# A four-layer graph network on one core: the candidate's aggregation side by seven products, and a new plan for the order of all queues

## The chip, the cores and the metric

The kernel runs on 1 core of one Trainium2 chip, in one launch. The metric is device time in microseconds (us), lower is better. Five queues work in it: PE (TensorE, matrix products), DVE (VectorE), ACT (ScalarE), POOL (GpSimd) and SP (SyncE, which issues nearly all transfers). Each executes its own instructions strictly in the order in which the program holds them; between queues only semaphores order the work.

## The reference

128 graphs of 128 nodes with 256 features each, float32, and an integer adjacency matrix per graph. Four layers, each `x = layernorm(x + gnn(x, adj))`:

```python
# layer 0: four edge scores, softmax, weighted sum
alpha = where(adj == k + 1, leaky_relu(einsum('bid,bjd->bij', x * a_k, x)), -9e15)   # k = 0..3
out0 = softmax(alpha) @ x
# layer 1: mean over neighbours
out1 = relu(x @ W_upd + (A^T (x @ W_msg)) / deg + bias)
# layer 2: three steps of a gated unit (GRU), weights w_ih, w_hh of 3 x 256 rows
for i in range(3):
    aggr = A^T (h @ weight[i])
    gi, gh = aggr @ w_ih.T + b_ih, h @ w_hh.T + b_hh
    r, z = sigmoid(i_r + h_r), sigmoid(i_z + h_z)
    n = tanh(i_n + r * h_n)                       # the candidate
    h = (1 - z) * n + z * h
# layer 3: attention with one vector, softmax, elu
out3 = elu(softmax(where(adj > 0, leaky_relu(f_i + f_j), -1e9)) @ (x @ W))
```

## The kernel before

**Work and tiles.** Four graphs make a group of 512 nodes (`G`, `T`), so there are 32 groups. In the three GRU steps the state lies transposed, as two tiles `hT[0]`, `hT[1]` of 128 features x 512 nodes. `weights` sets up: it turns the weights and multiplies `weight[i]` into `w_ih` (`c_gi`), so that aggregation comes first in each step (`aggregate`: 24 small bf16 products of the split state with the 0/1 matrix `a_ne`, copied to `agT` by ScalarE).

**Seven products instead of eight.** A gate (R, Z or the hidden side of the candidate C) is a 256 x 256 matrix times a 256 x 512 state. Read as 2 x 2 blocks, this is eight block products of 256 columns (or four products of 512 columns); `gate` makes it with seven, after Winograd. `sums` makes the four sums of state blocks (`t_h` on GpSimd from the state, `t_m` on VectorE from `agT`), the set-up the sums of weight blocks (`w_sh`, `w_sm`). The seven products accumulate in two PSUM banks: in `shared`, products 1, 6, 7 and 4 are added one after the other into the same columns, and after 1, after 6 and after 7 a `snapshot` copies the columns out before the next product adds to them; `other` holds products 2, 5 and 3. `added` brings snapshot and second bank together. So a gate has turns in which TensorE adds a product, ScalarE copies, and TensorE may go on only after the copy.

**One step** (`step`), in the order of its statements: the hidden side of the candidate `q` (seven products), aggregation, gate R with both sides (14 products, tile `t_r`), the candidate's aggregation side by `direct` (four products of 512 columns into two `ps` banks), `candidate` for the halves 1 and 0, gate Z with both sides (14 products, `t_z`), and `update`, which writes the new state, transposes it through DRAM (`turned`, `back`) and splits it into bf16 parts for the next step. In `candidate`, VectorE multiplies `t_r` by `q` and adds the `ps` bank, ScalarE takes tanh (`t_n`), GpSimd subtracts (`t_d`).

**The order of the queues** is neither the order of the statements nor written out by hand. Every call is recorded as an `Op`, and a planner at the end of the kernel (the loop over `left`, lines 970 to 1007) simulates the five engines with assumed costs and issues one operation after the other: of those that could start, the one with the earliest due time. Costs are the functions `pe_cost` to `pool_cost`, `LANDING` for transfers, and `HOP`, `PE_HOP`, `SLACK` for the way of a result to the next engine. Due times come from `paced`: each stage of group g gets a start and an end in periods (`PERIOD` = 82.744 us). In GRU steps only TensorE's operations spread the due times, and the other engines' are pulled forward by `EAGER`. `holds` models VectorE and GpSimd keeping each other off. The planner also decides when each rotating buffer is taken. All engine instructions are issued at line 232, which is why every row of the profile names L232; one goes by tiles.

**Buffers the change touches.** `h0T` (4 tiles, states from layer 1) and `hT` (6 tiles, states from the steps); `gate` (4 PSUM banks) and `ps` (4 PSUM banks); `w_sm` with sums for two gates.

Of the kernel before, what the change touches and what calls it, by code (L numbers as in the profile page):

```python
# [9 lines left out]
U8 = mybir.dt.uint8  # L10
I32 = mybir.dt.int32
BF16 = mybir.dt.bfloat16
# [6 lines left out]
def kernel(  # L19
# [38 lines left out]
    nc = tc.nc  # L58
# [84 lines left out]
    FAST = ("tensor_scalar", "tensor_scalar_add", "tensor_scalar_mul")  # L143

# [10 lines left out]
    class Op:  # L155
        def __init__(self, engine):
            self.engine, self.calls, self.took, self.landing = engine, [], 0.0, 0.0
            self.after, self.bufs, self.waiting = {}, [], 0
            self.ready, self.nominal, self.urgent = 0.0, 0.0, False
            self.waits = self.holds = False  # L160
            self.rush = 0.0

    class Engine:
# [24 lines left out]
        def __getattr__(self, name):  # L188
            def call(*args, **kw):
                op = self.group or self.record()  # L190
                named = dict(kw)
                out = [named.pop("out")] if "out" in named else [args[0]]
                rest = args if "out" in kw else args[1:]
                if "accum_out" in named:
                    out.append(named.pop("accum_out"))
                out = [v for v in out if isinstance(v, View)]
                ins = [v for v in (*rest, *named.values()) if isinstance(v, View)]
                n = 1
                for v in out + ins:
                    n = max(n, m_of(v))  # L200
                short = self is PE and BF16 in [v.buf.dtype for v in ins]
                op.took += SPLIT if short else self.cost(name, n, "accum_out" in kw)
                op.landing = LANDING if name == "dma_start" else 0.0

                tensors = [v for v in ins if m_of(v) > 4]
                if self is POOL:
                    op.waits, op.holds = True, name == "memset" or len(tensors) > 1
                elif self is DVE and name not in ("transpose", "bn_stats"):
                    op.waits = op.holds = not any(v.buf.pool is psum for v in out + tensors) and (
                        len(tensors) > 1 or (name in FAST and m_of(out[0]) > 4)  # L210
                    )
                for views, writes in ((ins, False), (out, True)):
                    for v in views:
                        whole = v.buf.pool is psum
                        for other, box, wrote in v.buf.accesses:
                            if other is not op and (writes or wrote) and (
                                whole or all(a < d and c < b for (a, b), (c, d) in zip(box, v.box))
                            ):
                                other.after[id(op)] = op
                for views, writes in ((ins, False), (out, True)):  # L220
                    for v in views:
                        v.buf.accesses.append((op, v.box, writes))
                        if v.buf not in op.bufs:
                            op.bufs.append(v.buf)
                            v.buf.left += 1
                op.calls.append((name, args, kw))

            return call
# [10 lines left out]
    LANDING = 4.2  # L239
    HOP = 0.235  # L240
    PE_HOP = 0.55
    SLACK = 0.873

    def pe_cost(op, n, sums):
        return 0.11 if op == "transpose" else 0.222 if n <= P else 0.003 + n / 599.0

    SPLIT = 0.056

    def dve_cost(op, n, sums):
        return 0.14 + n * (0.00056 if op in FAST else 0.00106)  # L250

    def act_cost(op, n, sums):
        return 0.6 if op == "dma_start" else 0.17 + n * 0.001 + (0.2 if sums else 0.0)

    def pool_cost(op, n, sums):
        return 0.2 + n * 0.00266 if op in FAST else 0.55 if op == "memset" else 1.2 if n < 64 else 0.25 + n * 0.0023

# [4 lines left out]
    SP = Engine("SP", nc.sync, lambda op, n, sums: 0.6)  # L262
# [3 lines left out]
    PERIOD = 82.744  # L266
    SPAN = 2.0
    EAGER, RUSH = 5.34, 0.516
    L0_START, L0_END, L1_START, L1_END, L3_START, L3_END = -2.032, -1.293, -0.75, -0.05, 0.173, 0.919
    H_END, M_START, M_END = 0.179, 0.179, 0.503  # L270

    def paced(start, end, pe_only=False):

        took = [op.took if not pe_only or op.engine is PE else 0.0 for op in line]
        total, sofar = sum(took), 0.0
        for op, t in zip(line, took):
            op.nominal = (start + (end - start) * sofar / total) * PERIOD
            op.urgent = pe_only
            sofar += t
        line.clear()  # L280

# [24 lines left out]
    w_sm = tile_of("w_sm", [P, NL, 3, 2, P])  # L306

    def weights():
# [3 lines left out]
        for src, tag, bufs in ((w_ih, "hT", 6), (w_hh, "rest", 4)):  # L312
            for g in range(0, NGC, 2):
                nat = tile_of(tag, [P, 2, D], bufs)
                ACT.dma_start(out=nat, in_=src[g * P : (g + 2) * P].rearrange("(g p) d -> p g d", p=P))
                nats.append(nat)
            if src is w_ih:
                for i in range(NL):
                    w = tile_of("hn", [P, KC, D], 3)
                    ACT.dma_start(out=w, in_=weight[i].rearrange("(c p) e -> p c e", p=P))  # L320
                    wnat.append(w)
        paced(-2.6, -2.5)
        for k, a in enumerate((a0, a1, a2, a3)):
            SP.dma_start(out=acol[:, k, :], in_=a.rearrange("(c p) -> p c", p=P))
        paced(-2.2, -2.1)
# [8 lines left out]
        paced(-2.0, -1.5)  # L334
# [22 lines left out]
        for i in range(NL):  # L357
            wT = tile_of("h0T", [P, KC, D], 4)
# [23 lines left out]
        for n in range(NL + 1):  # L382
            by, gates = POOL if n > 1 else DVE, 3 if n == 0 else 2
            w = [
                (w_hhT[:, k] if n == 0 else c_gi[:, n - 1, k])[:, : 2 * gates * P].rearrange(
                    "p (g e x) -> p g e x", [P, gates, 2, P], g=gates, e=2
                )
                for k in range(KC)
            ]
            w_s = w_sh if n == 0 else w_sm[:, n - 1]  # L390
            a11, a12, a21, a22 = w[0][:, :, 0], w[1][:, :, 0], w[0][:, :, 1], w[1][:, :, 1]
            s2, s3, s4 = [w_s[:, j] for j in range(3)]
            by.tensor_sub(s3, a11, a21)
            by.tensor_add(a21, a21, a22)
            by.tensor_sub(s2, a21, a11)
            by.tensor_sub(s4, a12, s2)
# [22 lines left out]
        paced(-1.9, -0.2)  # L419
# [88 lines left out]
    def loading(g, s):  # L508
# [12 lines left out]
        paced(g - 2.4, g - 2.1)  # L521
        SP.dma_start(out=s.x, in_=x[graphs].rearrange("b n d -> n b d"))
        paced(g - 1.9, g - 1.8)
# [67 lines left out]
    def layer1(g, s):  # L591
# [37 lines left out]
        for c in range(KC):  # L629
            t = tile_of("h0T", [P, T], 4)  # L630
# [12 lines left out]
    def gru(g, s):  # L643
# [5 lines left out]
        def step(i, hT, parts):  # L649
# [16 lines left out]

            def direct(w, v, q, ps=None, of=(0, 1), stop=True):

                start = ps is None
                ps = ps or bank("ps" if q >= C else "gate")  # L670
                with PE:
                    for k in of:
                        PE.matmul(
                            ps, w[:, k, q * P : (q + 1) * P], v[k],
                            start=(start and k == of[0]), stop=(stop and k == of[-1]),
                        )
                return ps
# [25 lines left out]
            def gate(tag, q, sources, copied, added, last=None):  # L703
# [14 lines left out]
                def snapshot(quarter):  # L718
                    copied(t[:, quarter], shared[:, :H], quarter // 2)
                    ops[-1].rush = RUSH  # L720
# [36 lines left out]
            def candidate(c, ps, t, q):  # L757
                DVE.scalar_tensor_tensor(t, t, 1.0, q, op0=OP.add, op1=OP.mult)
                DVE.tensor_add(t, t, ps)
# [6 lines left out]
            def update(c, z, n, d):  # L766

                DVE.scalar_tensor_tensor(d, z, 1.0, d, op0=OP.add, op1=OP.mult)
                new[c] = tile_of("hT", [P, T], 6)
# [12 lines left out]
            at = g + i * SPAN / NL  # L782
# [3 lines left out]
            paced(at, at + H_END, True)  # L786
            aggregate(0)
            aggregate(1)
            paced(at + M_START - 0.03, at + M_START, True)
            of_m = sums(DVE, agT, w_i, w_sm[:, i], agps, "t_m")  # L790
            t0, t1 = gate("t_r", R, (of_h, of_m), copy, DVE.tensor_add, tanh(R))
            n1, d1 = candidate(1, direct(w_i, agT, C + 1), t1, q1)
            n0, d0 = candidate(0, direct(w_i, agT, C), t0, q0)
# [3 lines left out]
            paced(at + M_START, at + M_END, True)  # L797
# [105 lines left out]
    for g in range(NG):  # L903
# [3 lines left out]
        paced(g + L0_START, g + L0_END)  # L907
        layer1(g, s)
        paced(g + L1_START, g + L1_END)
        gru(g, s)  # L910
        if g < NG - 1:
            layer3(g, s, 0, G)
            paced(g + SPAN + L3_START, g + SPAN + L3_END)
        else:

            for b in range(0, G, 2):
                layer3(g, s, b, b + 2)
                paced(g + SPAN + L3_START, g + SPAN + L3_END)
# [29 lines left out]
    def start_of(op):  # L948

        at = op.ready  # L950
        if op.waits:
# [19 lines left out]
    while left:  # L971
        best = None
        for e in engines:
# [5 lines left out]
            if best is None or at < best[0]:  # L979
                op = min(  # L980
                    (op for t, op in starts if t <= at),
                    key=lambda op: op.nominal - (EAGER if op.urgent and e is not PE else 0.0) - op.rush,
# [9 lines left out]
        e.free = at + op.took  # L992
        if op.holds:
            e.held = e.free - 0.14
        end = e.free + op.landing
# [3 lines left out]
        for other in op.after.values():  # L999
            other.waiting -= 1  # L1000
            hop = 0.0 if other.engine is e and not op.landing else SLACK if not other.urgent else HOP
            if hop == HOP and other.engine is PE:
                hop = PE_HOP
            other.ready = max(other.ready, end + hop)
# [31 lines left out]
```

## Time and profile before

| | |
|---|---|
| device time, median of 3 runs | 2764.06 us (2762.44 to 2764.56) |
| span of the profiled execution, first to last instruction | 2761.8 us, 2.3 us below that median |
| mean granted TensorE clock in it | 0.991 |
| busy: PE, DVE, ACT, POOL | 2702.3, 2304.1, 1584.2, 1666.2 us |
| candidate's aggregation side on PE (ps<-agT,c_gi) | 768 instructions of 512 columns |
| candidate's last addition on DVE (t_r<-t_r,ps) | 192 instructions, 131.4 us |

The profile has no device time of its own for the profiled execution; its span is what the rows add up to. A row of a group reads: line, engine, operation, written tile <- read tiles, shape, count, then busy time of all, mean of one in ns, and the idle time of that engine just before them with what ended it. PE is the row of matrix products, PEld that of weight loads; a float32 product counts as two instructions on each. Chain pieces and timeline rows begin with their start and length in us.

### The profile page before, as it was taken

What the parts mean: (1) busy time and instruction counts of PE and PEld (TensorE: products, weight loads), DVE (VectorE), ACT (ScalarE), POOL (GpSimd) and SP (SyncE); (2) the same over time, 40 slices, a digit from 0 to 9 for tenths busy, and PEclk for the clock granted to TensorE, in tenths of its full rate; (3) what the DMA queues carried; (4) which work ended last, traced back from release to release, by engine and by line L of the source; (5) the groups of instructions that cost most, each with busy time, mean ns of one, the idle gap of its engine ahead of it and who ended that gap; (6) DMA issues with size and microseconds to landing.
All of it is one profiled execution on the core that took longest, in us unless ns stands there. A gap on an engine that the chain in (4) does not pass through costs nothing.

```text
span 2761.8 us, 44048 instructions
## 1 busy us (share of the span) xinstructions
PE 2702.3 (98%) x13756; PEld 2138.1 (77%) x13756; DVE 2304.1 (83%) x5108; ACT 1584.2 (57%) x3704; POOL 1666.2 (60%) x1606
## 2 busy tenths in 40 slices
PE   8899999999999999999999999999999999999996
PEld 5677787887887887887887887887887887787774
DVE  5787888888888888888888888888888898888875
ACT  4454665555665655665655665655665655665554
POOL 4544666655666655666655666655676655675542
PEclk9999999999999999999999999999999999999996
DMA  5545555555555556555655556655556555545441
GB/s 121 129 90 99 115 126 129 120 109 124 122 125 131 121 108 129 118 124 133 121 107 127 121 121 134 121 110 123 121 121 134 124 109 120 116 110 118 99 88 43
DMA packets 1397130, 321.88 MB, mean 117 GB/s; under 512 B 1142560, under 2 KB 1388448, under 8 KB 1396896
## 3 DMA queue, kind: packets, MB, share of 16 engines
q1 hardware_dynamic: 1394448, 316.69, 53.7%
q10 hardware_dynamic: 2448, 2.36, 0.3%
q8 instruction: 111, 1.82, 0.3%
q14 instruction: 123, 1.01, 0.1%
HBM read 185.74 MB, written 133.15 MB: 115 GB/s over the span
## 4 chain that ended last, share of the span: by engine, by line
PE 94%; DVE 3%; POOL 1%; ACT 1%; DMA 1%; issue 1%; ACTq 0%; POOLq 0%; DVEq 0%; SPq 0%
PE gate L232 52%; PE ps L232 42%; DVE t_r L232 0%; POOL t_h L232 0%; DVE xb L232 0%; DVE st L232 0%; DMA rest<-in_L_gnn_w_hh_dram 0%; DVE z L232 0%; POOL rstd L232 0%; DMA hn<-in_L_gnn_weight_dram 0%; POOL xa L232 0%; DVE xa L232 0%; DVE t_d L232 0%; POOL t_d L232 0%; DVE hT L232 0%
## 5 line engine op out<-in xcount | busy, mean ns | idle before, releaser
L232 ACT ACTIVATE q<-gate,bhn 128x256 f32<-128x256 f32 x384 | 183.0, 477 | 314.4 <-PE gate L232 313.1
L232 PE MATMUL ps<-agT,c_gi 128*128 128x512 f32 x768 | 356.0, 592 | 0.0
L232 PE MATMUL gate<-t_h,w_hhT 128*128 128x256 f32 x1152 | 345.2, 381 | 5.7 <-ACT t_z L232 4.3
L232 PE MATMUL gate<-t_h,w_sh 128*128 128x256 f32 x1152 | 337.1, 383 | 4.2 <-ACT q L232 1.7
L232 POOL TENSOR_TENSOR rstd<-rstd,neg_half 128x4 f32<-128x4 f32 (+1 forms) x128 | 142.4, 1112 | 218.2 <-DVE rstd L232 215.1
L232 PEld LDWEIGHTS gate<-t_h,w_sh 128*128 128x128 f32 x1152 | 213.7, 191 | 62.8 <-issue 30.4
L232 PEld LDWEIGHTS ps<-xs,xT 128*128 128x128 f32 x2048 | 249.7, 193 | 11.5 <-ACT xs L232 2.6
L232 PEld LDWEIGHTS gate<-t_h,w_hhT 128*128 128x128 f32 x1152 | 211.7, 191 | 56.1 <-issue 16.3
L232 PE MATMUL ps<-xs,xT 128*128 128x128 f32 x2048 | 251.8, 276 | 2.2 <-ACT xs L232 1.3
L232 ACT COPY t_z<-gate 128x256 f32<-128x256 f32 x288 | 107.1, 372 | 244.6 <-PE gate L232 244.0
L232 PE MATMUL ps<-w_um,x1T 128*128 128x512 f32 x512 | 237.1, 595 | 0.2 <-ACT x1T L232 0.2
L232 PEld LDWEIGHTS ps<-agT,c_gi 128*128 128x128 f32 x768 | 145.8, 190 | 114.5 <-issue 106.0
L232 PE MATMUL gate<-agT,c_gi 128*128 128x256 f32 x768 | 229.2, 380 | 2.6 <-ACT agT L232 2.6
L232 PE MATMUL gate<-t_m,c_gi 128*128 128x256 f32 x768 | 228.5, 379 | 0.0
L232 PE MATMUL gate<-t_m,w_sm 128*128 128x256 f32 x768 | 228.4, 379 | 0.0
L232 PE MATMUL gate<-hT,w_hhT 128*128 128x256 f32 x768 | 222.8, 385 | 5.6 <-DVE hT L232 5.6
L232 POOL TENSOR_SCALAR mk<-a_f 128x512 uint8<-128x512 f32 x128 | 201.3, 1579 | 12.2 <-DVE alpha L232 6.6
L232 ACT ACTIVATE xs<-xT,acol 128x512 f32<-128x512 f32 x256 | 182.1, 717 | 40.9 <-PE ps L232 31.5
L232 POOL MEMSET hu<- 128x1 f32 x128 | 10.3, 96 | 303.8 <-DVE fac L232 224.5
L232 DVE TENSOR_TENSOR t_z<-gate,t_z 128x256 f32<-128x256 f32 x192 | 104.2, 543 | 101.4 <-ACT t_z L232 53.7
L232 POOL TENSOR_TENSOR t_d<-h0T,t_n 128x512 f32<-128x512 f32 x64 | 82.9, 1295 | 174.0 <-ACT t_n L232 171.1
L232 PEld LDWEIGHTS gate<-hT,w_hhT 128*128 128x128 f32 x768 | 141.8, 191 | 48.1 <-issue 23.6
(197 smaller groups left out, 7280.1 us busy)
## 6 DMA issues: line engine op xcount, KB each, us to landing
way_h<-z SPq DMA_DIRECT2D x190, 256.0 KB, 2.4
hn<-way_h SPq DMA_DIRECT2D x760, 64.0 KB, 2.4
way<-z SPq DMA_DIRECT2D x126, 256.0 KB, 3.2
x_blocks<-in_x_dram SPq DMA_DIRECT2D x256, 64.0 KB, 2.3
x_in<-in_x_dram SPq DMA_DIRECT2D x32, 512.0 KB, 3.8
way_x<-xb SPq DMA_DIRECT2D x32, 512.0 KB, 2.9
way_p<-z SPq DMA_DIRECT2D x62, 256.0 KB, 2.6
probT<-way_p SPq DMA_DIRECT2D x248, 64.0 KB, 2.3
```

The lines of the kernel that those rows point to most:

```text
L232: getattr(self.engine, name)(*[a.real() if isinstance(a, View) else a for a in args], **{k: a.real() if isinstance(a, View) else a for k, ...
```

## The change

- The candidate's aggregation side is made by `gate` with the seven products, from the sums `t_m` that gates R and Z use. It gets a tile `t_i` (four quarters of 256 columns) and two banks of `gate`, in place of `direct` and its two banks of `ps`. `w_sm` gets sums for the third gate.
- Its snapshots are ScalarE copies; its two inner additions are on VectorE.
- The candidate's last addition, `t_r` + `t_i`, moves from VectorE to GpSimd, except in the last group.
- States of layer 1 and of the steps share one pool of 9 tiles (`hT`) in place of 4 and 6.
- The planner gets other costs for every operation, other hops and margins, other due times for each stage, and a table of shifts for the first and the last six groups. It now tells when an engine is free (`took`) from when a result is there (`lasts`), and any operation that is not a holder no longer waits for the other engine's hold.

```diff
-    LANDING = 4.2
-    HOP = 0.235
-    PE_HOP = 0.55
-    SLACK = 0.873
-    def pe_cost(op, n, sums):
-        return 0.11 if op == "transpose" else 0.222 if n <= P else 0.003 + n / 599.0
-    SPLIT = 0.056
-    def act_cost(op, n, sums):
-        return 0.6 if op == "dma_start" else 0.17 + n * 0.001 + (0.2 if sums else 0.0)
...
+    LANDING = {"e": 5.66, "adj_in": 4.0, "x_in": 3.85, "x1T": 3.53, "way_1": 3.2, "way_2": 3.0, "xc": 3.6, "way_f": 2.0}
+    def pe_cost(op, n, out, ins, pointers, sums):
+        split = any(v.buf.dtype == BF16 or v.steps[-2:-1] == (("bitcast", (BF16,), {}),) for v in ins)
+        took = 0.11 if op == "transpose" else 0.056 if split else 0.005 + m_of(out[0]) / 600.0
+        return took, took + 0.165
...
+    def act_cost(op, n, out, ins, pointers, sums):
+        if op == "dma_start":
+            return 0.6, 5.0
+        lasts = 0.162 + n * 0.00083 + 0.1 * pointers
+        return lasts - 0.104 + (0.12 if sums else 0.0), lasts + (0.11 if sums else 0.0)
...
-    PERIOD = 82.744
-    SPAN = 2.0
-    EAGER, RUSH = 5.34, 0.516
-    L0_START, L0_END, L1_START, L1_END, L3_START, L3_END = -2.032, -1.293, -0.75, -0.05, 0.173, 0.919
-    H_END, M_START, M_END = 0.179, 0.179, 0.503
+    PERIOD = 81.79179
+    EAGER, RUSH = 5.2738, 1.1029
+    HOP, PE_HOP, SLACK, DMA_SLACK = 0.0939, 0.1018, 0.3009, 1.3133
+    TIMES = {
+        "loading": ((-269.2967, -216.6761), (-147.1123, -150.2193),),
+        "layer0": ((-168.1668, -107.0143),),
+        "layer1": ((-61.9931, -4.1582),),
+        "step0": ((2.1812, 23.4244), (7.0732, 27.4940), (15.2942, 41.6915),),
+        "step1": ((54.2807, 63.4509), (58.3678, 71.2000), (69.7980, 95.8240),),
+        "step2": ((108.6644, 125.1873), (123.1454, 127.3808), (118.2039, 151.9648),),
+        "layer3": ((179.8737, 241.5870),),
+    }
+    HEAD = (
+        (-59.717, -8.177, -28.638, -27.470, -4.121, 7.325, -10.397),
...
+    TAIL = (
+        (15.020, 3.976, 3.394, 9.445, 1.940, 13.363, 1.456),
...
-    w_sm = tile_of("w_sm", [P, NL, 3, 2, P])
+    w_sm = tile_of("w_sm", [P, NL, 3, 3, P])
...
-            t = tile_of("h0T", [P, T], 4)
+            t = tile_of("hT", [P, T], 9)
...
-            def direct(w, v, q, ps=None, of=(0, 1), stop=True):
...
-            def candidate(c, ps, t, q):
+            def candidate(c, aggregated, t, q):
                 DVE.scalar_tensor_tensor(t, t, 1.0, q, op0=OP.add, op1=OP.mult)
-                DVE.tensor_add(t, t, ps)
+                (DVE if g == NG - 1 else POOL).tensor_add(t, t, aggregated)
...
-                new[c] = tile_of("hT", [P, T], 6)
+                new[c] = tile_of("hT", [P, T], 9)
...
             t0, t1 = gate("t_r", R, (of_h, of_m), copy, DVE.tensor_add, tanh(R))
-            n1, d1 = candidate(1, direct(w_i, agT, C + 1), t1, q1)
-            n0, d0 = candidate(0, direct(w_i, agT, C), t0, q0)
+            i0, i1 = gate("t_i", C, (of_m,), copy, DVE.tensor_add)
+            n1, d1 = candidate(1, i1, t1, q1)
+            n0, d0 = candidate(0, i0, t0, q0)
...
-        if op.waits:
+        if op.holds:
             at = max(at, (POOL if op.engine is DVE else DVE).held)
...
+        end = at + op.lasts + (DMA_SLACK if op.dma else 0.0)
         if op.holds:
-            e.held = e.free - 0.14
-        end = e.free + op.landing
+            e.held = at + op.lasts - 0.12
...
-            hop = 0.0 if other.engine is e and not op.landing else SLACK if not other.urgent else HOP
-            if hop == HOP and other.engine is PE:
-                hop = PE_HOP
-            other.ready = max(other.ready, end + hop)
+            to_pe = other.engine is PE
+            if e is PE and to_pe:
+                ready = e.free
+            elif e is other.engine and not op.dma:
+                ready = end
+            else:
+                ready = end + (SLACK if not other.urgent else PE_HOP if to_pe else HOP)
+            other.ready = max(other.ready, ready)
```

## The prediction

> **What bounds the kernel now.** I read the page first (busy time, slices, chain), then the busy time stretch by stretch, then the chain in order of time, then the timeline of TensorE, then the groups by shape, then the waits.
>
> ```profile
> span 2761.8 us, 44048 instructions
> PE 2702.3 (98%) x13756; PEld 2138.1 (77%) x13756; DVE 2304.1 (83%) x5108; ACT 1584.2 (57%) x3704; POOL 1666.2 (60%) x1606
> ...
> PE 94%; DVE 3%; POOL 1%; ACT 1%; DMA 1%; issue 1%; ACTq 0%; POOLq 0%; DVEq 0%; SPq 0%
> ```
>
> 98% busy alone could hide waits, and 83% on VectorE is not far off. The busy time by stretches (columns: PE, PEld, DVE, ACT, POOL, clock, DMA share, GB/s) settles it:
>
> ```profile
> 0.00:85.00 85.00, 69.44 (x368) 51.03 (x369) 52.48 (x132) 36.28 (x78) 45.42 (x56) 0.98 0.59 132
> ...
> 1020.00:1360.00 340.00, 340.00 (x1774) 272.37 (x1773) 294.12 (x652) 202.59 (x473) 218.14 (x209) 1.00 0.57 121
> ...
> 2700.00:2762.00 62.00, 36.12 (x135) 25.18 (x135) 33.43 (x87) 29.15 (x76) 11.71 (x12) 0.72 0.13 35
> ```
>
> All six stretches from 340 to 2380 us read 340.00 of 340.00 on PE, at a granted clock of 1.00: 2040 us without an empty moment. What PE lacks lies at the ends: 22.5 us before 340 (340 - 317.5) and 37.2 us after 2380 (382 - 344.8). The chain in order of time gives the period of one group, by the same run of 28 product instructions in neighbouring groups:
>
> ```profile
> 1016.82 6.04 PE gate L232 x28
> ...
> 1099.49 6.04 PE gate L232 x28
> ```
>
> The period is 82.67 us and one 256-column product instruction takes 6.04 / 28 = 0.2157 us. The timeline gives the 512-column one, start to start:
>
> ```profile
> 1411.76 1.88 PE L232 MATMUL ps<-w_um,x1T 128*128 128x512 f32 x4
> 1413.48 0.59 PE L232 MATMUL gate<-t_h,w_hhT 128*128 128x256 f32 x2
> 1413.91 1.88 PE L232 MATMUL ps<-w_um,x1T 128*128 128x512 f32 x4
> 1415.62 0.59 PE L232 MATMUL gate<-t_h,w_sh 128*128 128x256 f32 x2
> ```
>
> 1.72 and 1.71 us for four, so 0.429 us each (the 0.59 us behind a pair of 256 contains the drain, which the next product covers). So in the middle the time is the number of product instructions times these pitches, and nothing else.
>
> **The products.** Each float32 product is two instructions. The candidate's aggregation side was 4 products of 512 columns per step: 8 x 0.429 = 3.43 us. It becomes 7 of 256: 14 x 0.2157 = 3.02 us. That is 0.41 us less per step, 1.24 us per group (period 82.67 to 81.43) and, over 96 steps, 768 x 0.429 - 1344 x 0.2157 = 329.5 - 289.9 = 39.6 us. 2040 / 82.67 = 24.7 of the 32 groups lie where PE is full (30.5 us certain); the other 9 us count where PE is busy, 92% of both ends (662 of 722 us). I take **-39 us**, bounds -30.5 and -39.6. That smaller products might be held up by their weight loads is excluded by the groups: the loads take 0.19 us each and the 28 in a row above still ran at 0.2157.
>
> **The other engines.** The rows by shape:
>
> ```profile
> L232 ACT COPY t_r<-gate 128x256 f32<-128x256 f32 x288 | 107.6, 374 | 91.5 <-PE gate L232 86.0
> L232 DVE TENSOR_TENSOR t_r<-t_r,ps 128x512 f32<-128x512 f32 x192 | 131.4, 684 | 8.3 <-PE ps L232 0.6 <-PE gate L232 0.5
> L232 DVE TENSOR_TENSOR t_r<-gate,t_r 128x256 f32<-128x256 f32 x96 | 39.3, 409 | 25.8 <-ACT t_r L232 24.4 <-PE gate L232 1.2
> L232 POOL TENSOR_TENSOR t_d<-hT,t_n 128x512 f32<-128x512 f32 x128 | 163.3, 1295 | 21.0 <-ACT t_n L232 21.0
> L232 DVE SCALAR_TENSOR_TENSOR t_r<-t_r,q 128x512 f32<-128x512 f32 x192 | 133.0, 693 | 13.3 <-ACT t_r L232 13.3
> L232 DVE SCALAR_TENSOR_TENSOR t_d<-t_z,t_d 128x512 f32<-128x512 f32 x192 | 174.4, 920 | 3.0 <-ACT t_z L232 3.0
> ```
>
> ScalarE gains 4 snapshots a step: 384 x 0.374 = 144 us, per period 49.2 + 12 x 0.374 = 53.7 of 81.4 us. VectorE loses 192 additions of 0.684 (131 us) and gains 96 of 0.409, 96 of about 0.69 and the last group's 6: 109.6 us; per period 71.5 to 70.8. GpSimd gains 186 additions at the 1.295 us of its nearest row: 241 us, 53.0 to 60.8 per period. None reaches 81.4, so all this hides under PE.
>
> GpSimd's additions touch VectorE all the same. The two last rows are the same operation on the same size in SBUF, 693 and 920 ns, and GpSimd works beside both: VectorE is held up at places by 0.2 us. If the 114 us by which the affected rows (t_d, the new hT, the second split) stand above 0.69 us grow with GpSimd's time (241 / 1666), that is 16 us, 0.5 per period. The Trainium skill ("SBUF — State Buffer", section "Who interferes with whom") speaks against the move: a GpSimd operation that reads SBUF and a VectorE one with two SBUF inputs lock each other out for a whole instruction. By that rule up to 7.8 us per period would be added to VectorE. With or without it, the worst case by rows, every one of 6 x 1.295 us standing still on VectorE, is 78.6 of 81.4: still not the bound, so 0 in the sum, but near enough to be a rival below.
>
> **The longer chain.** Candidate: VectorE multiply, GpSimd addition (+0.61 us against VectorE), ScalarE tanh, GpSimd subtraction; two halves, so GpSimd is taken 4 x 1.295 = 5.2 us. The z gate, 14 products of both sides, that is 28 instructions and 6.04 us on PE, stands beside it, and the update needs z anyway. Cost 0 in the middle; at the ends, where PE does wait, at most 0.61 x 2 halves x 3 steps = 3.7 us. Behind a GpSimd addition that waits for VectorE stand the next sums t_h and the powers of the normalisations; GpSimd now waits 218 us in front of those powers, so it has the room. The third gate's table in the set-up makes 12 operations half longer again (8 on GpSimd, 0.72 us before), under 4 us; 9 state buffers instead of 4 + 6 can hold VectorE's state write, where the row of hT shows 2.3 us idle in all: 0 taken, to 5. SP's transfers are the same in number and size.
>
> **The order.** The planner's costs and due times change all queues, and this decides the rest. In the listing of both programs' order with their waits, I took each product that waits for a ScalarE snapshot of the bank it adds to, and summed the TensorE work between the product snapshotted and the waiting one. Before, 49 such turns have 0.87 us or less: one in each middle period, 0.87 each, and the rest at the ends. After, there are 280: t_i 75, t_r 77, t_z 59, q 69. Six of these, with 0.43 or 0, lie in the middle. What a turn needs, the timeline shows near the end, where PE waits:
>
> ```profile
> 2694.37 0.63 PE L232 MATMUL gate<-t_h,w_sh 128*128 128x256 f32 x1
> 2695.04 0.47 ACT L232 ACTIVATE q<-gate,bhn 128x256 f32<-128x256 f32 x1 [2.28 <-PE gate L232]
> 2695.57 1.22 PE L232 MATMUL gate<-t_h,w_sh 128*128 128x256 f32 x2 [0.56 <-ACT q L232]
> ```
>
> The product ends at 2695.00 and the next starts at 2695.57. With the drain (0.59 - 0.43 = 0.16) a turn needs 0.72 us for q, and 0.62 for a 0.374 us copy. 0.86 is enough by 0.14 to 0.24 us if ScalarE is free at that moment. The six without cover cost 2 us (two at 0.62 and 0.72, four at 0.2 to 0.3). For the 226 more turns at 0.86: nothing each, if they go like the 25 before, which cost no slice of the middle anything; or, if ScalarE (66% taken, a mean instruction of 0.43 us) is met at random, 0.66 x 0.25² / (2 x 0.43) = 0.048 us, 11 us; or 0.66 x (0.72 - 0.24) each, 72 us, if a 0.72 us tanh always stands ahead. I take 5, nearer to the row of before, and with the six **+7 us**. At the ends, 14 turns have no cover after and 15 before: I take 0, bounds -25 and +15.
>
> **Sum.** 2761.8 - 39 + 7 = 2729.8 us of span. The median of the runs is 2764.06, 2.3 above the profiled span; with it, **2732 us**.
>
> **Rivals.** (A, 0.62) PE stays full, as summed: 2732, between 2715 and 2750. (B, 0.15, slower) ScalarE's queue becomes the clock: a snapshot stands behind a tanh that waits for VectorE. Rows for it: ScalarE idles 71.0 us before 96 such tanh of t_r, 0.74 each. If a third of the 226 turns lose that, it is 75 x 0.74 = 55 us: 2764 - 39 + 2 + 55 = 2782. It decides from 0.16 us per turn (37 / 226). Against it: the 25 tight turns of before. (C, 0.14) The new order also fills the ends; if it takes 25 of the 59.7 us that PE is empty there, 2707. Against it: as many uncovered turns there. (D, 0.09) GpSimd's additions make VectorE late: at 78.6 of 81.4 us each late result costs PE 0.7 us per period, 2755. That the products are not fewer is excluded by the listing (1344 instructions for 768).
>
> **How the numbers follow.** This kernel's measurement tells 0.2%, 5.5 us. Faster: A, C and half of D, 0.81. Same: some of D and of B's lower end, 0.06. Slower: 0.13. The range 2700 to 2768 takes in A, most of C, all of D and leaves out most of B.
>
> **What would show it.** Right: stretches in the middle again full on PE, equal runs 81.4 us apart, no group ps<-agT,c_gi, GpSimd t_r<-t_r,t_i x186 near 1.3 us, waits of PE gate for t_i, t_r, t_z and q below 20 us together. Wrong: middle stretches short of full, with PE waiting for ScalarE (B) or VectorE (D); or ends that differ by over 15 us (C).

## The result and the profile after

The changed kernel takes 2773.7 us (median of 6 runs, 2769.1 to 2774.8) against 2764.3 for the kernel before, measured beside it (6 runs, 2762.4 to 2765.4): a ratio of 1.003, interval 1.0019 to 1.0042. It is slower by 0.3%, where 2732 was forecast, with a range of 2700 to 2768. All issuing is at line 228 now, so the rows name L228.

The page of the kernel after (span, busy time, chain):

```profile
span 2771.3 us, 45549 instructions
PE 2689.0 (97%) x14332; PEld 2235.5 (81%) x14332; DVE 2211.5 (80%) x5114; ACT 1698.1 (61%) x4088; POOL 1929.6 (70%) x1792
...
PE 67%; DVE 15%; POOL 6%; ACT 4%; DMA 3%; issue 3%; SPq 2%; DVEq 0%; POOLq 0%; ACTq 0%
```

PE is busy for less time and the span is longer. The chain left PE: 94% of it was PE's before, 67% now, with 15% on VectorE. The same three stretches (PE, PEld, DVE, ACT, POOL, clock, DMA share, GB/s):

```profile
0.00:85.00 85.00, 69.12 (x357) 51.42 (x358) 49.60 (x129) 34.87 (x75) 45.71 (x55) 0.98 0.57 128
...
1020.00:1360.00 340.00, 334.28 (x1808) 281.40 (x1807) 275.62 (x642) 211.77 (x513) 246.01 (x229) 0.99 0.57 121
...
2700.00:2772.00 72.00, 41.28 (x154) 28.99 (x154) 36.14 (x97) 33.98 (x88) 18.12 (x19) 0.71 0.20 47
```

The middle is no longer full: over its six stretches PE is busy 2015.2 of 2040 us, where it was 2040.0.

**A better measure than busy time.** A product's record goes on for its drain, 0.16 us past the start of the next product, so a gap shorter than that does not show as idle. I went over the trace from start to start: each product's start, less the start of the product before it, less that one's pitch (0.216, 0.429, 0.056 us for a bf16 one); what is over is a late start. Between 340 and 2380 us these sum to 8.4 us before (150 steps from a bf16 to a float32 product at 0.056 each, no wait) and 58.5 us after: 99 products that wait for another engine, 38.2 us; in 101 cases the second instruction of a late product, 0.104 us in most, 10.7 us in all; and 9.6 us of type steps and small change, about 1 us of it products at half the granted clock (below).

This closes the account. All products at their pitches are 2679.3 us before and 2639.5 after (-39.8). What the spans hold beyond is 82.5 and 131.8 us (+49.3), of which the middle is 8.4 and 58.5 (+50.1) and the two ends together 74.1 and 73.3 (-0.8). So the products bring what was forecast, the ends change nothing in sum, and the middle gives back 50 us.

By the engine whose result let the late product go, the waits in the middle are: VectorE 20 us, ScalarE 11, GpSimd 7. The answer for the waits of PE on the gates (us, times, longest) shows the part of it that is visible as idle:

```profile
PE gate L228 <- DVE t_r L228: 6.3, 6, 2.6
PE gate L228 <- POOL t_h L228: 5.7, 10, 0.8
PE gate L228 <- ACT q L228: 4.6, 7, 1.2
PE gate L228 <- ACT t_z L228: 4.2, 9, 0.8
PE gate L228 <- DVE q L228: 4.0, 8, 0.9
```

No single engine is behind it. Behind one of the longest stands a chain, in the timeline of the kernel after, around 1180 us:

```profile
1180.46 0.69 DVE L228 TENSOR_TENSOR rest<-hn 128x512 f32<-128x512 f32 x1 [2.82 <-DMA hn<-way_h]
...
1183.03 0.42 DVE L228 TENSOR_TENSOR hu<-ps,bias_row 128x256 f32<-128x256 f32 x1
1183.36 0.68 DVE L228 TENSOR_REDUCE nmax<-alpha 128x4 f32<-128x512 f32 x1
1183.95 0.42 DVE L228 TENSOR_TENSOR t_r<-gate,t_r 128x256 f32<-128x256 f32 x1
...
1184.43 0.79 PE L228 MATMUL gate<-hT,w_sh 128*128 128x256 f32 x1 [2.64 <-DVE t_r L228]
```

Read it from below. Product 3 of gate R, which goes into the same columns of `other` as products 2 and 5, waits 2.64 us until VectorE has added snapshot and bank together (`added`; t_r<-gate,t_r). That addition had its inputs by 1180.47, when ScalarE's snapshot was done, 3.5 us before it began. But VectorE executes in order, and it had stood still for 2.82 us (from 1177.64) at the split of a state that was not yet back from DRAM; all that the plan had put between split and addition came late by that. The wait costs more than itself: from 1183.88 us the granted clock is 0.5 for 3.4 us, and the next products start 0.427 us apart where 0.216 is usual, some 1.4 us more. A stretch (its clock is the third number from the end) and two rows of the timeline show it:

```profile
1183.00:1187.00 4.00, 2.57 (x6) 2.13 (x7) 3.35 (x15) 2.90 (x11) 4.00 (x4) 0.61 0.22 35
...
1185.44 1.06 PE L228 MATMUL gate<-agT,w_sm 128*128 128x256 f32 x2
...
1187.65 0.59 PE L228 MATMUL gate<-t_m,c_gi 128*128 128x256 f32 x2
```

The SP queue shows why the split was late:

```profile
1170.58 3.14 SPq L228 DMA_DIRECT2D rT<-way  x2
1173.83 0.50 SPq L228 DMA_DIRECT2D x_in<-in_x_dram  x1
1174.43 2.87 SPq L228 DMA_DIRECT2D hn<-way_h  x4
1177.40 1.12 SPq L228 DMA_DIRECT2D way_h<-z  x1
```

The four issues of `hn` alone take 2.87 us, behind others in the same queue, and VectorE is at the split before the last has landed. By its numbers the new plan allows a part of `hn` 3.7 us from its planned issue (2.4 for the landing and 1.31 of `DMA_SLACK`), and 96 of the 760 took longer in the trace; the plan of before allowed 4.8 (0.6 and 4.2), and 7 took longer. Over the whole kernel the split shows what was new in the row that had no idle time before (busy, mean ns, idle time before it); with it the other rows that the prediction had costed:

```profile
L228 DVE TENSOR_TENSOR rest<-hn 128x512 f32<-128x512 f32 x128 | 101.6, 795 | 13.6 <-DMA hn<-way_h 13.3
L228 POOL TENSOR_TENSOR t_r<-t_r,t_i 128x512 f32<-128x512 f32 x186 | 245.4, 1332 | 106.0 <-ACT t_i L228 73.0
L228 ACT COPY t_i<-gate 128x256 f32<-128x256 f32 x384 | 142.5, 371 | 92.0 <-PE gate L228 87.1
L228 DVE SCALAR_TENSOR_TENSOR t_d<-t_z,t_d 128x512 f32<-128x512 f32 x192 | 166.5, 875 | 45.9 <-ACT t_z L228 33.9 <-POOL t_d L228 8.0 <-POOL t_h L228 3.9
```

Following each of the 99 waits back through what its releaser had waited for, 16.9 of the 38.2 us end at a late `hn`, 17.6 at TensorE itself (turns that the order made too tight) and 3.7 stayed unresolved. This is argued from the trace; e6 below tests the part of `hn`, and nothing tests the other two apart.

### The profile page after: what moved, and what is told of

It reads as the page before. It is cut to its first block, busy times and chain, and to the rows that moved or that the text cites. A ratio compares the mean times of both kernels' runs of the same rounds, so it can differ in the third digit from the quotient of the medians.

```text
span 2771.3 us, 45549 instructions
## 1 busy us (share of the span) xinstructions
PE 2689.0 (97%) x14332; PEld 2235.5 (81%) x14332; DVE 2211.5 (80%) x5114; ACT 1698.1 (61%) x4088; POOL 1929.6 (70%) x1792
## 4 chain that ended last, share of the span: by engine, by line
PE 67%; DVE 15%; POOL 6%; ACT 4%; DMA 3%; issue 3%; SPq 2%; DVEq 0%; POOLq 0%; ACTq 0%
PE gate L228 45%; PE ps L228 22%; SPq L228 2%; DMA hn<-way_h 2%; DVE z L228 2%; DVE rest L228 2%; DVE st L228 1%; POOL t_r L228 1%; DVE t_d L228 1%; DVE t_r L228 1%; DVE hT L228 1%; DVE xb L228 1%; POOL t_h L228 1%; POOL t_d L228 1%; DVE t_m L228 1%
## 5 line engine op out<-in xcount | busy, mean ns | idle before, releaser
L228 PE MATMUL gate<-t_h,w_hhT 128*128 128x256 f32 x1152 | 347.4, 385 | 11.3 <-ACT t_z L228 3.5
L228 PE MATMUL gate<-t_h,w_sh 128*128 128x256 f32 x1152 | 344.7, 384 | 5.5 <-ACT q L228 2.5
L228 PE MATMUL gate<-t_m,w_sm 128*128 128x256 f32 x1152 | 340.2, 380 | 3.1 <-DVE t_m L228 1.6
L228 PE MATMUL gate<-t_m,c_gi 128*128 128x256 f32 x1152 | 341.8, 379 | 0.2 <-ACT t_i L228 0.2
L228 PE MATMUL gate<-agT,c_gi 128*128 128x256 f32 x1152 | 337.3, 381 | 1.3 <-DVE q L228 0.7
L228 PE MATMUL gate<-hT,w_hhT 128*128 128x256 f32 x1152 | 331.3, 382 | 3.2 <-DVE hT L228 1.6
L228 POOL TENSOR_TENSOR t_r<-t_r,t_i 128x512 f32<-128x512 f32 x186 | 245.4, 1332 | 106.0 <-ACT t_i L228 73.0
L228 POOL TENSOR_TENSOR rstd<-rstd,neg_half 128x4 f32<-128x4 f32 (+1 forms) x128 | 150.3, 1175 | 240.5 <-DVE rstd L228 221.6
L228 POOL TENSOR_TENSOR t_d<-hT,t_n 128x512 f32<-128x512 f32 x192 | 254.3, 1337 | 26.8 <-ACT t_n L228 24.5
L228 PEld LDWEIGHTS gate<-t_h,w_hhT 128*128 128x128 f32 x1152 | 206.2, 190 | 72.4 <-issue 26.3
L228 PEld LDWEIGHTS ps<-xs,xT 128*128 128x128 f32 x2048 | 250.0, 194 | 12.0 <-ACT xs L228 2.3
L228 PE MATMUL ps<-xs,xT 128*128 128x128 f32 x2048 | 254.5, 278 | 3.1 <-DVE xa L228 1.1
L228 PEld LDWEIGHTS gate<-t_h,w_sh 128*128 128x128 f32 x1152 | 210.9, 190 | 56.3 <-issue 14.6
L228 PEld LDWEIGHTS gate<-t_m,w_sm 128*128 128x128 f32 x1152 | 218.0, 190 | 39.1 <-ACT t_i L228 4.4
L228 PEld LDWEIGHTS gate<-hT,w_hhT 128*128 128x128 f32 x1152 | 215.4, 191 | 37.8 <-issue 4.2
L228 PEld LDWEIGHTS gate<-t_m,c_gi 128*128 128x128 f32 x1152 | 218.3, 190 | 34.1 <-issue 2.6
L228 PEld LDWEIGHTS gate<-agT,c_gi 128*128 128x128 f32 x1152 | 217.1, 190 | 35.4 <-DVE q L228 2.8
L228 ACT ACTIVATE q<-gate,bhn 128x256 f32<-128x256 f32 x384 | 182.0, 474 | 95.7 <-PE gate L228 91.4
L228 PE MATMUL ps<-w_um,x1T 128*128 128x512 f32 x512 | 239.3, 593 | 0.6 <-DVE xb L228 0.6
L228 POOL TENSOR_SCALAR mk<-a_f 128x512 uint8<-128x512 f32 x128 | 209.5, 1643 | 22.6 <-DVE alpha L228 14.7
L228 ACT ACTIVATE xs<-xT,acol 128x512 f32<-128x512 f32 x256 | 178.2, 719 | 67.7 <-PE ps L228 49.8
L228 DVE SCALAR_TENSOR_TENSOR t_d<-t_z,t_d 128x512 f32<-128x512 f32 x192 | 166.5, 875 | 45.9 <-ACT t_z L228 33.9
```

The source lines that it names most:

```text
L228: getattr(self.engine, name)(*[a.real() if isinstance(a, View) else a for a in args], **{k: a.real() if isinstance(a, View) else a for k, ...
```

## The experiments

My theory after the result: the products are cheaper as computed, and the order of the queues loses the 50 us, by results that reach TensorE a little late. Rivals put the loss on one thing: on the addition on GpSimd, on transfers that the planner thinks too fast, on the hops and margins (0.09 to 0.30 us, where 0.24 to 0.87 stood), or on the seven products themselves, under any order. Ratios below are against the kernel before, run beside each.

**The new work under the old plan.** Kernel before, with the third gate by seven products and one pool of 9 states; last addition on VectorE (e1), and on GpSimd (e2):

```diff
+            i0, i1 = gate("t_i", C, (of_m,), copy, DVE.tensor_add)
-            n1, d1 = candidate(1, direct(w_i, agT, C + 1), t1, q1)
+            n1, d1 = candidate(1, i1, t1, q1)
...
-                DVE.tensor_add(t, t, aggregated)
+                (DVE if g == NG - 1 else POOL).tensor_add(t, t, aggregated)   # e2 only
...
```

> The kernel before with its own plan, and the candidate by seven products (i gate, snapshots on ScalarE), last addition on VectorE, one pool of 9 states (two pools do not fit beside the new tile). Theory M (the new plan leaves too little margin: the 50 us by which products start late in the middle of the changed kernel come from its order): the middle stretches are full again, 2764 - 39 = about 2726 us. Theory P (the products themselves: three more turns per step through four banks and ScalarE stall TensorE under any order): about 2770. Theory G (the addition on GpSimd makes GpSimd and then VectorE late): it is absent here, 2726.

> As e1, with the last addition on GpSimd as in the changed kernel, still with the plan of before. Theory M: like e1, about 2727 us. Theory P: about 2770. Theory G: e1 plus the 40 to 50 us, about 2770, with TensorE waiting for t_h of GpSimd and for VectorE.

Measured: e1 2815.3 (1.0189, 1.0172 to 1.0206), e2 2863.0 (1.0359, 1.0344 to 1.0374). The seven products, planned with the old costs, lose 51 us, and 99 with the addition on GpSimd. No theory had e1 above 2770. Late starts in the middle are 77.8 and 117.7 us, and the ends grow by some 20 and 29 us. The 48 us from e1 to e2 are what the theory of the addition on GpSimd (G) had named, but the order was made anew between them too, so they don't tell the addition from the order. The old plan could not carry the seven products, and the new plan is worth 89 us to the work of the changed kernel (2863.0 to 2773.7).

**The old work under the new plan** (e3): the changed kernel with `direct` and the last addition on VectorE, as before. The weight block of the third gate holds a sum for the seven products, so the candidate's numbers are others; amount and kind of work are those of the kernel before, but for the third gate's sums in the set-up and the one pool of 9 states.

```diff
-            i0, i1 = gate("t_i", C, (of_m,), copy, DVE.tensor_add)
-            n1, d1 = candidate(1, i1, t1, q1)
+            n1, d1 = candidate(1, direct(w_i, agT, C + 1), t1, q1)
...
```

> The changed kernel with its new plan and pool, but the candidate's aggregation side by four products of 512 columns and the last addition on VectorE, as before. Theory M: the late starts stay, 2764 + 40 = about 2805 us, PE short of full in the middle. Theory P and theory G: they go, about 2764 us, PE full.

Measured: 2786.6 (1.0081, 1.0066 to 1.0096). The work of the kernel before, in an order made with the new plan's numbers, takes 22 us more than in its own: 41.8 us of late starts in the middle for 8.4, less 11 us at the ends. The rival that the products alone are at fault falls: the new plan makes late starts with the old work too. They are other ones, though. Some 15 us of the waits are for ScalarE's t_z, which lets go 2.3 us of them in the changed kernel.

**The margins** (e4), and **the margin of transfers alone** (e8):

```diff
-    HOP, PE_HOP, SLACK, DMA_SLACK = 0.0939, 0.1018, 0.3009, 1.3133
+    HOP, PE_HOP, SLACK, DMA_SLACK = 0.235, 0.55, 0.873, 1.3133   # e4
+    HOP, PE_HOP, SLACK, DMA_SLACK = 0.0939, 0.1018, 0.3009, 2.7   # e8
```

> The changed kernel with one line altered: the planner's HOP, PE_HOP and SLACK back to 0.235, 0.55 and 0.873 us (new costs and due times kept). Theory M: the turns get cover, most of the 50 us in the middle go, 2725 to 2735 us. Theory P and theory G: 2770 or more, TensorE late as before.

> The changed kernel with one number of the planner altered: the allowance on top of a transfer's landing (DMA_SLACK) 2.7 instead of 1.3133 us, which is about what the plan of before allowed; a new order follows. Theory T: the late starts go, 2740 or less. Theory G: no difference, 2773. Theory Q: the order is another one with its own uncovered turns, anywhere from 2755 to 2800, with the late starts on other lines.

Measured: e4 2794.7 (1.011, 1.0095 to 1.0125), e8 2795.1 (1.0112, 1.0097 to 1.0127), both 21 us slower than the changed kernel, about half of it in the middle and half at the ends. The theories of margins (M, for e4) and of transfers (T, for e8) had 2740 or less. The waits of VectorE for `hn` in e8:

```profile
DVE rest L228 <- DMA hn<-way_h: 0.3, 1, 0.3
```

13.3 us of such waits are down to 0.3, exactly as meant, yet the late starts in the middle rise from 58.5 to 68.4: the order that comes out has other tight turns (ScalarE's t_z 11 us, GpSimd's t_h 10). A number changed in the planner changes the place of everything; it doesn't take away one wait. So neither run tells what a margin is worth, and the next three keep the order of the changed kernel fixed and change only what runs in it.

**The order kept, the addition back on VectorE** (e5). It is planned for GpSimd and issued on VectorE:

```diff
-                getattr(self.engine, name)(
+                getattr(getattr(op, "on", self).engine, name)(
...
                 (DVE if g == NG - 1 else POOL).tensor_add(t, t, aggregated)
+                ops[-1].on = DVE
```

> The changed kernel with every queue's order kept as it is (the planner still counts the addition as GpSimd's), but the candidate's last addition issued on VectorE at the same place. Theory G (the addition on GpSimd makes t_h and with it TensorE late, and holds VectorE up): the middle loses 20 us or more of its 50, 2750 or less. Theory T (transfers: the turned state lands late, and VectorE's split at the head of its queue keeps the gates' inner additions back): no gain, 2770 to 2780. Theory Q (queues: many small latenesses of all helpers, each met by an order without cover): a few us either way, 2765 to 2780.

Measured: 2774.8 (1.004, 1.0025 to 1.0055): the same as the changed kernel, with the late starts (56.5 us) too. The engine of the addition does not decide the time, in this order. VectorE's own operations do feel it: t_d, 875 ns in the changed kernel, has here

```profile
L228 DVE SCALAR_TENSOR_TENSOR t_d<-t_z,t_d 128x512 f32<-128x512 f32 x192 | 161.1, 846 | 45.1 <-ACT t_z L228 34.7 <-POOL t_d L228 5.1 <-POOL t_h L228 4.0
```

**The order kept, no split of a step's state behind a transfer** (e6): the splits for steps 2 and 3 read the state as VectorE wrote it, in place of its turned copy, so the numbers are others. All transfers are still made; the first step still has its state through DRAM. **Both** (e7).

```diff
-                ap = getattr(ap, name)(*a, **k)
+                ap = a[0].memory().rearrange("p (b n) -> p b n", b=G) if name == "other" else getattr(ap, name)(*a, **k)
...
-                    split_up[c] = split(turning[c], DVE)
+                    h = turning[c]
+                    split_up[c] = split(View(h.buf, h.shape, h.box, (("other", (new[c].buf,), {}),)), DVE)
```

> The changed kernel with every queue's order kept, but the splits of steps 1 and 2, and the aggregation behind them, read the state where VectorE wrote it and not the turned one that comes back through DRAM; the transfers still take place, and nothing but layer 3 waits for them. The aggregation of steps 2 and 3 is then made on the state not turned. Theory T: most of the 50 us go, 2735 or less. Theory Q: what the trace traces back to late transfers goes, 17 of 38 us of waits and their follow-ons, about 2750. Theory G: under 10 us, 2765 or more.

> e5 and e6 together, order kept, with e6's change of the aggregation's input. Theory T: as e6. Theory G: as e5 or below. Theory Q: the sum of both differences, about 2750, and still 20 us of late starts in the middle that neither transfer nor GpSimd's addition explains.

Measured: e6 2755.5 (0.9971, 0.9959 to 0.9983), e7 2764.8 (1.0001, 0.9992 to 1.0011). The stretch of e6 that read 334.28 on PE in the changed kernel:

```profile
1020.00:1360.00 340.00, 337.67 (x1842) 283.60 (x1841) 276.92 (x641) 217.04 (x526) 251.87 (x234) 1.00 0.58 122
```

Late transfers cost the changed kernel 18 us by the medians and 14 between the two profiled runs (2771.3 and 2757.4), where the tracing back gave 16.9. The waits let go by VectorE's t_r and q (with the short operation fac behind them) fall from 16.7 to 7.4 us, though VectorE's own work is the same: that part was the transfers' doing. Some 44 us of late starts stay. In e7 the addition on VectorE costs 9 us that it did not cost in e5, so the two effects do not add up; which result then comes late I have not traced.

**Other orders of the same work.** If the order is the cause, other numbers in the planner must move the time with the work unchanged. e9 is the changed kernel with the addition on VectorE, planned anew; e10 and e11 are e9 with other numbers; e12 is the work of the changed kernel to the instruction (addition on GpSimd) with other numbers:

```diff
-    PERIOD = 81.79179
-    EAGER, RUSH = 5.2738, 1.1029
-    HOP, PE_HOP, SLACK, DMA_SLACK = 0.0939, 0.1018, 0.3009, 1.3133
+    PERIOD = 81.8532   # e10; e11 82.9083; e12 83.0
+    EAGER, RUSH = 7.3065, 1.0538   # e11 7.7613, 1.2976; e12 7.4261, 1.4511
+    HOP, PE_HOP, SLACK, DMA_SLACK = 0.1521, 0.0977, 0.2421, 1.8593   # e11 0.0777, 0.1915, 0.1, 1.6359; e12 0.0722, 0.2481, 0.2312, 1.6359
...
-                (DVE if g == NG - 1 else POOL).tensor_add(t, t, aggregated)   # not e12
+                DVE.tensor_add(t, t, aggregated)
```

> The changed kernel with the last addition on VectorE, and the planner knowing it, so that a new order follows from the same numbers. Theory G (GpSimd's addition is the cost): 2750 or less. Theory Q (an order without cover, whatever the engines): 2755 to 2790.

> The same work as e9 (seven products, last addition on VectorE) in another order: the planner's numbers are EAGER 7.3065, RUSH 1.0538, PERIOD 81.8532 and HOP, PE_HOP, SLACK, DMA_SLACK 0.1521, 0.0977, 0.2421, 1.8593; costs and due times as in the changed kernel. Theory Q: the products' 39 us are there to be had once the helpers' gate work is pulled forward and transfers get more allowance; 2725 to 2750, with under 30 us of late starts in the middle. Theory P2 (three more turns per step lose what seven products gain, in any order): 2760 or more, the late starts on other lines.

> As e10 with a second set of numbers: EAGER 7.7613, RUSH 1.2976, PERIOD 82.9082, margins 0.0777, 0.1915, 0.1000, 1.6359. Theory Q: 2725 to 2755. Theory P2: 2760 or more.

> As e10 with the last addition on GpSimd, as in the changed kernel, and numbers that suit it: EAGER 7.4261, RUSH 1.4511, PERIOD 83.0, margins 0.0722, 0.2481, 0.2312, 1.6359. Theory Q: 2735 to 2765, between e10 and the changed kernel. Theory P2: 2765 or more. Theory G: 2770 or more.

| | median us | ratio, interval | late starts 340 to 2380 us | of it waits |
|---|---|---|---|---|
| before | 2764.4 | 1 | 8.4 | 0 |
| after | 2773.7 | 1.003 (1.0019 to 1.0042) | 58.5 | 38.2 (99) |
| e9 | 2778.2 | 1.005 (1.0035 to 1.0065) | 59.6 | 40.3 (93) |
| e10 | 2744.2 | 0.9927 (0.9912 to 0.9942) | 32.9 | 20.8 (64) |
| e11 | 2756.0 | 0.9969 (0.9957 to 0.9981) | 44.0 | 25.8 (83) |
| e12 | 2753.7 | 0.9961 (0.9947 to 0.9975) | 48.8 | 30.3 (107) |

e12 against the changed kernel is the plain test: the same instructions in another order, 20 us less. e9 against e10 is the other: 34 us less. Not all of it lies in the middle: between the profiled runs it is 16 us for e12, 10 in the middle and 6 or 7 at the ends, and 32 for e10, 27 and 5. And no order of the seven products that ran has less than 32.9 us of late starts, 24.5 more than before. So the order is shown to move 20 to 34 us; that the rest of the 50 can be had by an order too is not shown. e10 beats both kernels, by 20 us (0.7%) and by 29 us. Its page:

```profile
span 2742.8 us, 45630 instructions
PE 2676.5 (98%) x14332; PEld 2239.9 (82%) x14332; DVE 2318.8 (85%) x5300; ACT 1712.5 (62%) x4088; POOL 1711.9 (62%) x1606
...
PE 78%; DVE 12%; POOL 3%; DMA 3%; ACT 2%; issue 2%; SPq 1%; DVEq 0%; POOLq 0%; ACTq 0%
```

The split of the turned state in e10:

```profile
L228 DVE TENSOR_TENSOR rest<-hn 128x512 f32<-128x512 f32 x128 | 93.1, 728 | 0.0
```

And its chain of waits, the same run of 46 product instructions in neighbouring groups:

```profile
1006.61 9.93 PE gate L228 x46
...
1088.63 9.93 PE gate L228 x46
...
1170.63 9.93 PE gate L228 x46
```

VectorE never waits for `hn` there, and the order repeats from group to group, 82.0 us apart. In the chain of the changed kernel over the same 250 us no run of this length comes back. e10 keeps 19 of the 39.8 us by its span (2761.8 to 2742.8): 24.5 us are still lost in the middle, and the ends are 4 us shorter than before. VectorE, at 85%, is busier in e10 than in the changed kernel and still holds TensorE up less.

## Why the prediction was wrong

- **What bounds the kernel before**: right. There is not one wait in 2040 us, by starts too.
- **The products, -39**: right; -39.8 by pitches in the trace. That no product would be held up by a weight load held only where products follow each other without a wait (last section).
- **The other engines, 0**: the busy times came near the sums, but "so all this hides under PE" did not follow from them (the order, below). GpSimd's additions took the 1.3 us assumed (1332 ns). ScalarE and VectorE stayed below PE. One pool of 9 states did not hold VectorE's state write up: 1.0 us of idle time stands before the row of hT, 2.3 before. The 16 us by which GpSimd's additions were to lengthen VectorE's rows are there, when the order is kept: from the changed kernel to e5, all VectorE operations on 128x512 with two inputs in SBUF (the moved addition apart) take 23 us less, and the mean of t_d goes from 875 to 846 ns. That t_d had 920 ns before, with less work on GpSimd, shows that the order moves these rows as well. The rule of the Trainium skill ("SBUF — State Buffer", section "Who interferes with whom"), by which a GpSimd operation that reads SBUF and a VectorE one with two inputs in SBUF lock each other out, agrees with the changed kernel's trace: t_d, the new hT and t_r<-t_r,q took 0.64 to 0.71 us in the 155 cases with no GpSimd operation beside them, and 0.84 in the mean, up to 1.80, in the other 421. In time, the move is worth nothing in this order (e5), and in e7 the addition on VectorE costs 9 us.
- **The ends, 0**: right, -0.8, for this order; in other orders they moved by -11 (e3) to +29 us (e2).
- **The order, +7**: this is the step that failed. It measured +50. I had counted one kind of turn, product to ScalarE snapshot to next product. Those cost 10 to 11 us in all. That this is my bound by random meeting is luck: it was some 33 waits of 0.3 us, where the formula has a short delay at over a third of 226 turns. The test named for them held: PE's waits for ScalarE's t_i, t_r, t_z and q are 11.6 us, below 20. What was missing: turns over two engines, where product 3 waits for VectorE's inner addition and VectorE stands behind something else (20 us); GpSimd's sums t_h, first in the next step (7 us); the second halves of late products (11 us); and transfers. I had put SP's transfers at nothing since their number was the same, while the plan shortened the margin for their landing. e6 prices that at 14 to 18 us, most of it within VectorE's 20.
- **A, full in the middle**: fell. **B** said slower at 2782 by a queue that is late, and the sign and size came near by luck: the queue was VectorE's with transfers at its head, not ScalarE's behind a tanh. **C**: the ends did not fill. **D**: that VectorE is late was right, but not by GpSimd's additions (e5).
- **The error in method**: "PE was full before, so 25 tight turns cost nothing, so 226 will cost little" took a property of the old order for one of the turns. In the old order every result was in time. e3 shows that the same work loses 22 us in an order by the new plan. The listing of waits had shown that everything moved; of the many kinds of turn in it I counted the one that the change names.

What stays open: which order would have no late start with the seven products, if there is one (by the account it would take about 2725 us, 2764 less 39.8); which of the planner's many new numbers (costs, holds, due times, margins) made the turns tight, as each run that changed one made a whole new order; and why e6 and e5 together (e7) are worse than e6.

## What to carry to other kernels

When a change comes with a new order of in-order queues, cost the order first: list every kind of wait that ends at the bounding engine, over one and over two engines and over transfers, and look for how early each result is, not only for whether the engine was full before. An engine that is 20% idle can still hold up the bound, if what stands at the head of its queue is late. And to tell an order from the work in it, run the old work in the new order, and the new work in a fixed order with one dependence taken away: a changed planner number moves everything at once.

## What the hardware showed that I had not expected

- **A late product pays twice.** The second of the two instructions of a float32 product starts 0.104 us later than its pitch when the first had to wait: 101 cases in the changed kernel, 10.7 us. At 429.29 us in its trace the late first instruction's record is 0.48 us long, where 0.38 is usual; its second weight load ends at 429.58, and the second instruction starts at 429.61.
- **A long wait can cost clock as well.** The wait of 2.64 us at 1184 us is followed by products at half the granted clock, another 1.4 us for this one wait. It is the only such stretch between 340 and 2380 us in the changed kernel, and e6, which does not have this wait, has none.
- **The idle column sees half.** 24.8 us of idle time on PE in the middle, 58.5 us of late starts, since each gap below the 0.16 us drain is covered by the record.
- **A step from a bf16 to a float32 product costs 0.056 us**: the second instruction of the first float32 product starts late by that, 150 times in the middle of the kernel before, 8.4 us that no view shows as idle. The 150 steps the other way cost nothing.
- **Landing is uneven.** From issue to landing `hn` takes 2.52 us in the median, 3.90 in one of ten and 5.78 in one of a hundred (2.40, 3.58 and 4.66 before). A plan with a fixed number for it, 3.7 us here, is late at some places, and an in-order queue hands that on to all that stands behind.
